# Short sorting networks drawn as two-dimensional passes, key segments stored side by side, and one subtraction left out, in a two-layer graph kernel

## The chip, the cores and the metric

The kernel runs on one core of a Trainium2 chip. The metric is device time in microseconds (us) of one execution, so lower is better. "VectorE" below is the engine that the profile calls DVE, "GpSimd" is POOL, "ScalarE" is ACT, "TensorE" is PE, and SyncE (SP) issues the plain transfers.

## The reference, cut to what matters

There are 16 graphs of 1024 nodes with 64 channels each, a weighted adjacency matrix per graph, and a node mask.

```python
# layer 0: mean over the neighbours, weighted by the adjacency
h = relu(layernorm(x));  x = x + (adj / clip(adj.sum(-1), 1)) @ h
# layer 1: a sum of quantiles over the neighbours that are left
h = relu(layernorm(x))
nb = (adj > 0) off the diagonal;  m = nb.sum(-1)
# a node with m > 10 drops every ceil(m/2)-th neighbour, and the drop goes both ways
sv = sort over the left neighbours and the node itself, per channel, of h
agg = 0.25*quantile(sv, .25) + 0.5*quantile(sv, .5) + 0.25*quantile(sv, .75)
x = x + mask * (relu((h + agg) @ W1 + b1) @ W2 + b2)
```

The number of neighbours is very uneven: the first nodes of a graph have the most, up to some 90, and most nodes have fewer than ten.

## The kernel before, in words

**Layer 0** goes batch by batch, 16 times. SyncE loads adjacency tiles of 128x1024 (`at`). ScalarE takes their signs (`sg`, with row sums), TensorE transposes them and multiplies them with the normalised rows. VectorE multiplies the signs by descending column numbers and takes the 8 largest out of each of 4 segments with MAX8 (`rec`), so each node gets a list of at most 32 neighbours. The stream `endings` then sorts the 1024 nodes of a batch by class of length. The class is a one-hot tile `hot`; two matmuls put into PSUM, for each of 184 columns (23 classes by 8 tiles), how many nodes stand earlier in the tile and how many the column has; a running sum over the columns (TENSOR_TENSOR_SCAN into `base`), a subtraction that makes it exclusive, an addition, a product with `hot` and a reduction give each node's position. GpSimd scatters the node's row to that position in DRAM (`srt<-row,to`).

**Layer 1** works on four groups of four batches. In a group the sorted positions are 32 tiles of 128 nodes; tile 0 holds the longest, and the others take the first `CAPS` neighbours: 15, 10, 8, 7, 7, 6, and so on down to 1. Tiles of one length form a job (`Job`): n = cap + 1 rows to sort (the node itself is row 0), T tiles. The jobs of a group have (n, T) = (16,1), (11,1), (9,1), (8,2), (7,1), (6,4), (5,4), (4,6), (3,6), (2,5). GpSimd gathers the n - 1 neighbour rows, one DMA_INDIRECT of 128 rows each (`places<-tab,idx`; in the last group `last_idx`). VectorE marks dropped neighbours and sorts each channel with a network of elementwise min and max over whole rows of 64 columns: the `passes`. Only the lower three quarters of the sorted rows are needed. Then `weigh` multiplies the rows by their weights into `prod`, TensorE sums them and runs the two small matrix products, and GpSimd scatters the result (`out_dram<-y`).

A network is not done in place. Every row has two copies: copy 0 in the gathered SBUF tile `places`, copy 1 in a PSUM tile `other` (row 0 starts in a third, `S`). For each comparator a digit of a hand-kept table `GOES[n]` says into which copies its minimum and its maximum go. `network` collects the comparators of a layer that have the same operation, the same source copies, the same distance and the same destination copy, and a cover function packs their rows into passes: `runs_of` into arithmetic runs (one stride), `grids_of` into grids of two strides with at most `MOST` = 8 rows. Grids are used in layers with a rule from `GOES_LONG`, which the long lists have and the short jobs do not. `spread` orders the passes so that one that needs a fresh result is put later. The tile framework adds a semaphore wait wherever an instruction conflicts with an earlier one on a tile. There is one buffer of `other`, so the passes of two short jobs never mix.

**Long lists.** The first positions of each group hold nodes with 88, 28, 21 and 18 kept neighbours. For each of these four lists `long_lists` gathers full adjacency rows (`gat_rows`), builds one f16 key per column (`lkey`, 128x1024), takes 16 or 24 keys out of each of 8 segments with MAX8 and MATCH_REPLACE8 (`lfound`), then the largest of those (`lkeys`). Segment s is every eighth column from s on, and the key tile is stored in column order, so a segment is read with a stride of 8 elements (16 bytes). Its rows then go through networks of n = 89, 29, 22 and 19 (`lplaces`, with `l0other` or `lother` as the second copy, both in SBUF).

**Order of the work.** Nearly everything is emitted at build time by a planner (`Plan`): streams offer their next instruction with a rank, the planner keeps a clock per engine with assumed costs, and the stream that can begin earliest on its engine goes next, ties by rank. The order on VectorE and GpSimd is the emitted one. A VectorE pass is assumed to take 0.07 us plus 1.04 ns per column; a wait between two passes is not in these costs. `progress["ahead"]` counts gathers that are planned and not yet emitted; while it is under 16, sorts are put ahead of layer 0's VectorE work so that gather buffers (four of `places`) come free. All these instructions carry line 240 in the profile, that of the helper that records them, so groups are told apart by tile.

Of the kernel before, what the change touches and what calls it, by code (L numbers as in the profile page):

```python
# [15 lines left out]
OP = mybir.AluOpType  # L16
# [28 lines left out]
LSEG = 8  # L45
# [80 lines left out]
def numbers(run):  # L126
# [7 lines left out]
    2: "2",  # L134
    3: "302",
    4: "03110",
    5: "130330222",
    6: "112302211333",
    7: "0331030103122000",
    8: "2112033030321122333",  # L140
    9: "211232203032203001023303333",
    11: "1212120202301300132300022233211111010",
    16: "12121212302030200303200130031332000333111131312202220111330033",
}


# [5 lines left out]
}  # L152


def network(n, width, block=None):

    count = -(-3 * (n - 1) // 4) + 1  # L160
    live = set(range(count))
    layers = []
    block = block or n
    for layer in reversed(SHORT.get(n) or batcher(n)):
        kept = [(i, j, i in live, j in live) for i, j in layer if i in live or j in live]
        live.update(x for pair in kept for x in pair[:2])
        layers.append(kept)
    goes = iter(GOES.get(n, ()))
    rules = iter(GOES_LONG.get(n, "").split())
    at = [2] + [0] * (n - 1)  # L170
    ops = []
    for layer in reversed(layers):
        kinds, after = {}, {}
        inside = all(i // block == j // block for i, j, _, _ in layer)
        rule = dict(zip(sorted({(at[i], at[j]) for i, j, _, _ in layer}), next(rules, "")))
        for i, j, lo, hi in layer:
            ai, aj = at[i], at[j]
            other = (0 if ai == 1 else 1) + (0 if aj == 1 else 2)
            to = int(rule.get((ai, aj)) or next(goes, other))
            results = [(OP.min, i, to & 1)] * lo + [(OP.max, j, to >> 1)] * hi  # L180

            results.sort(key=lambda r: r[2] == at[r[1]])
            after.update({i: 0, j: 0})
            for turn, (op, x, copy) in enumerate(results):
                part = i // block if inside else -(-n // block)
                kinds.setdefault((part, turn, op == OP.max, ai, aj, j - i, copy), []).append(i)
                after[x] = copy
        for x, copy in after.items():
            at[x] = copy
        for (part, _, is_max, *kind), left in sorted(kinds.items()):  # L190
            cover = grids_of if rule else runs_of
            ops.extend(
                (part, (OP.max if is_max else OP.min, *kind, run)) for run in cover(left)
            )
    parts = [
        spread([op for p, op in ops if p == part], width) for part in range(1 + -(-n // block))
    ]
    return parts, count, at
# [187 lines left out]
def list_path(ctx, tc, x, adj, nodemask, w1, b1, w2, b2, out, go):  # L386
    nc = tc.nc
    B, N, C = x.shape
# [47 lines left out]
    zeros = zero.to_broadcast([P, N])  # L436
# [75 lines left out]
    nc = plan.nc  # L512
# [238 lines left out]
    def endings(pool, now):  # L751

        first = lambda rank: rank - 3000
        for b, st in enumerate(batch):
            now[0] = b
            g = max(g for g in range(NG) if FIRST[g] <= b)
            size = GROUPS[g]
            yield "ACT", lambda: known(st, "rec", "row") if st["listed"] == NT else INF
            rec, total, row = st["rec"], st["total"], st["row"]

            for t in range(NT):
                nc.scalar.activation(
                    row[:, t, R0:R0 + 8 * NSEG], rec[:, t, :], AF.Relu, bias=before[:, t:t + 1]
                )


            yield "DVE", always
            found = new(pool, [P, NT, 8 * NSEG], BF, "found", 1)
            nc.vector.tensor_scalar(found, rec, 0.0, None, op0=OP.is_gt)
            d = new(tiny, [P, NT], F32, "d", 2)  # L770
            nc.vector.tensor_reduce(d, found, AX.X, OP.add)
            full = new(tiny, [P, NT], F32, "full", 2)
            nc.vector.tensor_reduce(
                full, found.rearrange("p t (s e) -> p t s e", e=8)[:, :, :, 7], AX.X, OP.max
            )
            nc.vector.scalar_tensor_tensor(d, full, float(STEPS[0]), d, op0=OP.mult, op1=OP.max)
            nc.vector.tensor_scalar(d, d, float(STEPS[0]), None, op0=OP.min)
            for s in STEPS[1:]:
                nc.vector.scalar_tensor_tensor(d, total, float(s), d, op0=OP.is_gt, op1=OP.add)
            free(rec)  # L780
            free(total)
            hot = new(tiny, [P, CLS, NT], BF, "hot", 2)
            nc.vector.tensor_tensor(
                hot, cls, d.unsqueeze(1).to_broadcast([P, CLS, NT]), OP.is_equal
            )
            yield "PE", lambda: max(at(hot), room("ps_small", 3))
            pc = new(ps_s, [P, HALF], F32, "ps_small", 3, users=1)
            K = CLS * NT
            flat = hot.rearrange("p c t -> p (c t)")
            nc.tensor.matmul(pc[:, :K], earlier, flat, start=True, stop=True)  # L790
            nc.tensor.matmul(pc[:, K:2 * K], ones, flat, start=True, stop=True)
            yield "DVE", lambda: at(pc) + SLACK
            base = new(tiny, [P, K], F32, "base", 2)
            nc.vector.tensor_tensor_scan(
                base, pc[:, K:2 * K], zeros[:, :K], 0.0, op0=OP.add, op1=OP.add
            )
            nc.vector.tensor_tensor(base, base, pc[:, K:2 * K], OP.subtract)
            nc.vector.tensor_tensor(base, base, pc[:, :K], OP.add)
            free(pc)
            nc.vector.tensor_tensor(base, base, flat, OP.mult)  # L800
            pos = new(tiny, [P, NT], F32, "pos", 2)
            nc.vector.tensor_reduce(pos, base.rearrange("p (c t) -> p t c", t=NT), AX.X, OP.add)
            low = new(tiny, [P, NT], I32, "low", 2)
            nc.vector.tensor_copy(low, pos)
            nc.vector.tensor_scalar(low, low, LSUB - 1, None, op0=OP.bitwise_and)
            if size == 2:
                aside = new(tiny, [P, 2, NT], F32, "aside", 2)
                for e, by in enumerate((-32.0, 64.0)):
                    nc.vector.tensor_scalar(
                        aside[:, e, :], pos, 64.0 / (e + 1), by, op0=OP.is_lt, op1=OP.mult  # L810
                    )
                for e in range(2):
                    nc.vector.tensor_tensor(pos, pos, aside[:, e, :], OP.add)
            nc.vector.tensor_scalar(
                pos, pos, float(size), float(LSUB * (b - FIRST[g])), op0=OP.mult, op1=OP.add
            )
            to = new(pool, [P, NT], I32, "to", 2)
            nc.vector.scalar_tensor_tensor(to, low, float(1 - size), pos, op0=OP.mult, op1=OP.add)
            for t in range(NT):
                yield "POOL", lambda: max(at(to), at(row)) + LOOSE if "normed" in st else INF, first  # L820
                scatter(srt[g], row[:, t, :], to[:, t:t + 1], sorts[g])
            free(row)
            progress["batches"] = b + 1
# [21 lines left out]
    class Job:  # L845
# [190 lines left out]
        def sort(self):  # L1036
            n, T, pool, short, A, S = self.n, self.T, self.pool, self.short, self.A, self.S
# [10 lines left out]
                ok, self.keys.rearrange("p t k -> p k t"), 0.0, gone, op0=OP.is_gt,  # L1048
                op1=OP.subtract,
            )  # L1050
            self.ops, self.count, self.copies = network(n, T * C)
            self.counts(ok)

            vals = A[:, 1:, :, :].rearrange("p k t w -> p (k t) w")[:, :, :C]
# [5 lines left out]
                HUGE, vals, op0=OP.mult, op1=OP.add,  # L1060
# [263 lines left out]
    def long_lists(pool):  # L1324

        yield "DVE", always
        rev = new(pool, [P, N], HF, "rev", 1)
# [13 lines left out]
        for l in LORDER:  # L1341
            K = LONG[l]
# [21 lines left out]
                full, col_f, node, full, op0=OP.not_equal, op1=OP.mult  # L1364
            )
            key = new(pool, [P, N], HF, "lkey", 1)
            nc.vector.scalar_tensor_tensor(key, full, 0.0, rev, op0=OP.is_gt, op1=OP.mult)

            found = new(pool, [P, LSEG, max(LCAPS)], HF, "lfound", 1)
            found = found[:, :, :LCAPS[l]]  # L1370
# [1 line left out]
            for r in range(LCAPS[l] // 8):  # L1372
                for s in range(LSEG):
                    if s % 4 == 0:
                        yield "DVE", always
                    top = found[:, s, 8 * r:8 * r + 8]
                    seg = key.rearrange("p (q s) -> p s q", s=LSEG)[:, s, :]
                    if r:
                        nc.vector.match_replace(
                            out=seg, in_to_replace=last[s], in_values=seg, imm_value=0.0  # L1380
                        )
                    nc.vector.max(out=top, in_=seg)
                    last[s] = top
# [89 lines left out]
    nc = tc.nc  # L1473
# [291 lines left out]
```

## Time and profile before

| | |
|---|---|
| Median of 3 runs | 1470.73 us (1468.12 to 1472.69) |
| The profiled execution's own time | 1469.38 us |
| Its span, first to last instruction | 1467.6 us |
| VectorE busy | 1267.8 us (86%), 4263 instructions |
| GpSimd busy | 939.3 us (64%), 1112 instructions |
| ScalarE, TensorE busy | 577.8 us, 738.8 us |
| Mean granted TensorE clock | 0.707 |

Busy time counts an instruction from its start to its end. Consecutive VectorE instructions can overlap, and the short idle time that a wait between two of them leaves is not in the busy share. On GpSimd the profile's busy time of a gather is about 1 us, and another 0.3 us between two gathers is shown as idle with releaser "issue".

### The profile page before, as it was taken

Reading aid. Unit: us, or ns where it says so; the run is one execution under the profiler, and the core shown is the slowest. Engines: PE = TensorE matmul, PEld = TensorE weight load, DVE = VectorE, ACT = ScalarE, POOL = GpSimd, SP = SyncE. Lnnn points to the kernel's source line nnn. Section 1 sums busy time; section 2 is a strip of 40 time slices with the busy share of each in tenths; the row PEclk is TensorE's granted clock in tenths of the full one; section 3 lists DMA queues with packets and bytes.
Section 4 is the critical chain, followed back from the end, with each engine's and each line's share of the span. In section 5 each row is a group of like instructions: output and inputs, shape, how many; then the busy total and the mean of one; then the engine's idle time right before and its main releaser. Section 6 shows DMA issues by size and latency. Waiting matters only on the chain.

```text
span 1467.6 us, 14957 instructions
## 1 busy us (share of the span) xinstructions
PE 738.8 (50%) x3186; PEld 460.6 (31%) x3186; DVE 1267.8 (86%) x4263; ACT 577.8 (39%) x1747; POOL 939.3 (64%) x1112
## 2 busy tenths in 40 slices
PE   4778777228778347683585663200510101224864
PEld 2444334214445224352353332100410001123753
DVE  6878799999999895899959967588999998999895
ACT  7989879245666324783454432000100000000110
POOL 0132227777767777577876777477777787778432
PEclk9889898559989558895598676555665555555876
DMA  5446667424464224465233232321211111221000
GB/s 175 150 145 185 163 192 196 119 67 112 135 164 141 66 51 112 129 194 136 69 93 96 82 71 48 63 68 41 43 39 24 25 30 31 44 46 24 16 11 11
DMA packets 134591, 132.22 MB, mean 90 GB/s; under 512 B 100196, under 2 KB 102884, under 8 KB 134372
## 3 DMA queue, kind: packets, MB, share of 16 engines
q1 hardware_dynamic: 102972, 91.00, 21.6%
q0 software_dynamic: 31520, 40.19, 12.6%
q14 instruction: 72, 0.59, 0.1%
q8 instruction: 27, 0.44, 0.1%
HBM read 111.62 MB, written 23.61 MB: 92 GB/s over the span
## 4 chain that ended last, share of the span: by engine, by line
DVE 44%; POOL 19%; issue 11%; ACT 10%; DMA 9%; PE 5%; SPq 1%; DVEq 0%; POOLq 0%; ACTq 0%
POOL places L240 11%; DVE places L240 7%; DVE other L240 6%; DVE lplaces L240 5%; DVE rec L240 5%; DMA at<-in_adj_dram 4%; DMA places<-tab,idx 4%; POOL lplaces L240 4%; ACT sg L240 3%; PE pt L240 3%; ACT ln_sq L240 2%; DVE l0other L240 2%; DVE sg L240 2%; POOL out_dram L240 2%; PE ps_small L240 2%
## 5 line engine op out<-in xcount | busy, mean ns | idle before, releaser
L240 POOL DMA_INDIRECT places<-tab,idx x372 | 371.6, 999 | 115.5 <-issue 105.7
L240 PE MATMUL pt<-ident,prod 128*128 128x128 f32 (+1 forms) x736 | 162.5, 384 | 396.4 <-DVE prod L240 320.3
L240 PEld LDWEIGHTS pt<-ident,prod 128*128 128x128 f32 (+1 forms) x736 | 132.9, 264 | 428.1 <-issue 255.7
L240 PE MATMUL ps_small<-att,h 128*65 128x512 f32 x512 | 255.0, 645 | 14.1 <-ACT att L240 6.7
L240 POOL DMA_INDIRECT srt<-row,to x128 | 128.1, 1001 | 178.5 <-ACT row L240 156.0
L240 PE MATMUL pt<-ident,at 128*128 128x128 f32 x1024 | 167.1, 308 | 93.9 <-ACT att L240 71.7
L240 DVE MAX8 rec<-sg 128x8 f16<-128x256 f16 x512 | 180.2, 414 | 4.4
L240 PEld LDWEIGHTS pt<-ident,at 128*128 128x128 f32 x1024 | 128.0, 156 | 139.0 <-ACT att L240 95.3
L240 ACT ACTIVATE sg<-at 128x1024 f16<-128x1024 f32 x128 | 135.0, 1055 | 89.9 <-DMA at<-in_adj_dram 69.6
L240 POOL DMA_INDIRECT lplaces<-whole,lidx x125 | 132.1, 1057 | 38.3 <-issue 37.4
L240 POOL DMA_INDIRECT places<-tab,last_idx x124 | 126.2, 1018 | 37.8 <-issue 36.3
L240 ACT COPY att<-pt 128x512 f32<-128x512 f32 x256 | 141.4, 583 | 19.0 <-PE pt L240 17.6
L240 PEld LDWEIGHTS ps_small<-att,h 128*65 128x65 f32 x512 | 74.0, 151 | 148.2 <-issue 119.7
L240 ACT COPY ot<-pt 128x128 f32<-128x128 f32 (+3 forms) x56 | 22.4, 399 | 230.2 <-PE pt L240 228.1
L240 DVE TENSOR_TENSOR sg<-sg,keyed 128x1024 f16<-128x1024 f16 x128 | 87.3, 682 | 29.4 <-ACT sg L240 29.3
L240 POOL DMA_INDIRECT out_dram<-y,nodes_i x93 | 97.0, 1043 | 21.0 <-issue 13.9
L240 ACT ACTIVATE wu<-wu 128x39 f32<-128x39 f32 (+9 forms) x40 | 9.5, 237 | 255.2 <-DVE wu L240 255.2
L240 PE MATMUL ps_small<-ot,w_sb 128*128 128x128 f32 (+3 forms) x112 | 49.4, 531 | 100.4 <-DVE y L240 84.1
L240 ACT ACTIVATE hid<-ps_small,b_sb 128x128 f32<-128x128 f32 (+2 forms) x56 | 28.1, 504 | 126.3 <-PE ps_small L240 126.0
L240 DVE TENSOR_TENSOR other<-places,other 128x64 f32<-128x64 f32 (+6 forms) x204 | 69.4, 340 | 5.4
L240 DVE TENSOR_TENSOR places<-places,other 128x64 f32<-128x64 f32 (+2 forms) x208 | 62.3, 309 | 4.8
L240 DVE TENSOR_TENSOR places<-other,places 128x128 f32<-128x128 f32 (+5 forms) x160 | 54.9, 343 | 3.4
(269 smaller groups left out, 1651.3 us busy)
## 6 DMA issues: line engine op xcount, KB each, us to landing
at<-in_adj_dram SPq DMA_DIRECT2D x128, 512.0 KB
places<-tab,idx POOLq DMA_INDIRECT x372
whole<-tab SPq DMA_DIRECT2D x4, 1057.0 KB
tab<-row SPq DMA_DIRECT2D x16, 264.0 KB
xt<-in_x_dram SPq DMA_DIRECT2D x16, 256.0 KB
srt<-row,to POOLq DMA_INDIRECT x128
lplaces<-whole,lidx POOLq DMA_INDIRECT x125
places<-tab,last_idx POOLq DMA_INDIRECT x124
```

The lines of the kernel that those rows point to most:

```text
L240: ins = getattr(self._engine, op)(*args, **kwargs)
```

## The change

1. Five tables of `GOES` are new (n = 5, 7, 9, 11, 16): the min and max results of the comparators go to other copies than before.
2. For jobs of one tile (T = 1: n = 16, 11, 9, 7) `network` covers with `grids_of` in place of `runs_of`. The networks themselves, their comparators and the rows that they compare are the same. The lists of n = 29, 22, 19 go through the same call with `one` true; their passes stay as they are.
3. The long lists' key tile is written segment by segment, so that a segment's 128 keys are contiguous; the one instruction that writes the keys of a list now writes with a stride of 128 elements (256 bytes) from one key to the next.
4. In `endings` the scan starts one column later, behind a MEMSET of the first column, which makes the sum exclusive without the subtraction.

```diff
-    5: "130330222",
+    5: "110013113",
-    7: "0331030103122000",
+    7: "2110003230211333",
-    9: "211232203032203001023303333",
-    11: "1212120202301300132300022233211111010",
-    16: "12121212302030200303200130031332000333111131312202220111330033",
+    9: "121220200011112221230000333",
+    11: "1212101010001222211000022211100003333",
+    16: "12121212010301030000222022201111000000222222220000111111000000",
...
-def network(n, width, block=None):
+def network(n, width, block=None, one=False):
...
-            cover = grids_of if rule else runs_of
+            cover = grids_of if rule or one else runs_of
...
             base = new(tiny, [P, K], F32, "base", 2)
+            nc.vector.memset(base[:, :1], 0.0)
             nc.vector.tensor_tensor_scan(
-                base, pc[:, K:2 * K], zeros[:, :K], 0.0, op0=OP.add, op1=OP.add
-            )
-            nc.vector.tensor_tensor(base, base, pc[:, K:2 * K], OP.subtract)
+                base[:, 1:], pc[:, K:2 * K - 1], zeros[:, :K - 1], 0.0, op0=OP.add, op1=OP.add
+            )
             nc.vector.tensor_tensor(base, base, pc[:, :K], OP.add)
...
-            self.ops, self.count, self.copies = network(n, T * C)
+            self.ops, self.count, self.copies = network(n, T * C, one=T == 1)
...
             key = new(pool, [P, N], HF, "lkey", 1)
-            nc.vector.scalar_tensor_tensor(key, full, 0.0, rev, op0=OP.is_gt, op1=OP.mult)
+            segs = key.rearrange("p (s q) -> p s q", s=LSEG)
+            nc.vector.scalar_tensor_tensor(
+                segs.rearrange("p s q -> p q s"), full.rearrange("p (q s) -> p q s", s=LSEG), 0.0,
+                rev.rearrange("p (q s) -> p q s", s=LSEG), op0=OP.is_gt, op1=OP.mult,
+            )
...
-                    seg = key.rearrange("p (q s) -> p s q", s=LSEG)[:, s, :]
+                    seg = segs[:, s, :]
```

## The prediction

> **What bounds the kernel now.** I read the page's first two parts, then busy time by stage, then the vector engine's timeline inside one short job, then the rows of single tiles.
>
> ```profile
> PE 738.8 (50%) x3186; PEld 460.6 (31%) x3186; DVE 1267.8 (86%) x4263; ACT 577.8 (39%) x1747; POOL 939.3 (64%) x1112
> ...
> DVE  6878799999999895899959967588999998999895
> ACT  7989879245666324783454432000100000000110
> POOL 0132227777767777577876777477777787778432
> ...
> DVE 44%; POOL 19%; issue 11%; ACT 10%; DMA 9%; PE 5%; SPq 1%; DVEq 0%; POOLq 0%; ACTq 0%
> ```
>
> VectorE is busy nearly everywhere and carries 44% of the chain that ended last. GpSimd's 7s are not slack: between two gathers lie 0.3 us with the releaser "issue", so a gather costs 1.25 to 1.3 us and at most 39 fit into 50 us. Three stages by window:
>
> ```profile
> 200.00:915.00 715.00, 433.53 (x1848) 262.13 (x1847) 623.73 (x2102) 363.81 (x1105) 529.13 (x639) 0.76 0.42 112
> 915.00:1380.00 465.00, 107.63 (x499) 81.90 (x498) 416.93 (x1330) 26.70 (x70) 347.75 (x359) 0.56 0.19 39
> 1380.00:1467.60 87.60, 50.02 (x257) 39.96 (x256) 70.66 (x254) 9.83 (x26) 24.53 (x41) 0.71 0.03 10
> ```
>
> The waits of GpSimd have this row:
>
> ```profile
> POOL out_dram L240 <- DVE lrem L240: 22.9, 1, 22.9
> ```
>
> In the windows the columns are PE, PEld, DVE, ACT, POOL. In 200 to 915 (layer 0 with groups 0 to 2) VectorE is 87% busy; with its short waits between dependent instructions only some 50 us of the 715 are real idle. In 915 to 1380 (long lists, group 3) it is 34 of 465. GpSimd is full too: leaving out gaps under 0.4 us, it idles 58 us in all from 250 to 1375. But its last gather is issued at 1378, and then VectorE still has 71 us of sorting; the wait shows GpSimd standing 22.9 us for it. So the end is VectorE's backlog, with GpSimd close behind.
>
> **Where a short sort spends its time.** The timeline of VectorE in group 2's n = 16 job (start, us, instruction; "x2" are two merged):
>
> ```profile
> 768.79 0.30 DVE L240 TENSOR_TENSOR other<-places 128x128 f32<-128x128 f32 x1
> 769.13 0.22 DVE L240 TENSOR_TENSOR places<-other,places 128x64 f32<-128x64 f32 x1
> 769.27 0.47 DVE L240 TENSOR_TENSOR places<-places,other 128x128 f32<-128x128 f32 x2
> 769.78 0.23 DVE L240 TENSOR_TENSOR other<-other,places 128x64 f32<-128x64 f32 x1
> 770.04 0.29 DVE L240 TENSOR_TENSOR places<-places,other 128x128 f32<-128x128 f32 x1
> ```
>
> From 769.13 to 769.27 a 64-column pass takes 0.14 us, from 769.78 to 770.04 it takes 0.26. A free pass costs 0.07 us plus 0.067 per row of 64; one that waits for its predecessor starts 34 ns after that one's end and costs 0.12 more. I marked every pair of neighbouring passes in the 40 short jobs. A pass waits when it reads or writes `other` and the pass before it wrote `other`, or writes it and that one read it, **whatever the rows** (the PSUM tile is tracked as a whole); in `places` only when the rows themselves conflict. Of 605 pairs marked as conflicting 578 wait, of 195 marked free none does.
>
> [...]
>
> **Part 1, networks.** I worked the old and new tables through `network` and `spread`, counted passes, and waits by the rule above. Rows moved are unchanged (17, 31, 52, 72, 121 rows times T). Time is 0.07 x passes + 0.067 x rows x T + 0.12 x waits.
>
> | n (T) | passes | waits | us by rule | saved |
> |---|---|---|---|---|
> | 5 (4) | 16 to 14 | 13 to 9 | 7.2 to 6.6 | 0.6 |
> | 7 (1) | 22 to 20 | 16 to 12 | 5.5 to 4.9 | 0.6 |
> | 9 (1) | 38 to 29 | 28 to 20 | 9.5 to 7.9 | 1.6 |
> | 11 (1) | 43 to 32 | 30 to 19 | 11.4 to 9.3 | 2.1 |
> | 16 (1) | 63 to 36 | 51 to 21 | 18.6 to 13.1 | 5.5 |
>
> The trace has 18.9, 10.4 to 10.9, and 9.0 to 9.4 us for n = 16, 11, 9 before, so the rule is sound; where another job's instruction falls between two passes it hides a wait, and I take 40 us for four groups in place of 41.6. The rows' final copies also need fewer `prod` products: one less for n = 5, 9, 11, two for n = 16, at 0.07 us, 1.4 us in all. That a two-stride pass costs no more per row is read from the long lists, where such passes of 512 columns take 685 ns, as one-stride ones do; none touches PSUM yet. There are 24 two-stride passes a group. Below, they cost nothing more (each row is still 64 contiguous columns), or gain; above, take the 13 ns by which 64-column passes on `other` alone last longer than on `places` first (232 against 219), 96 times: 1.2 us. I take nothing.
>
> **Part 2, keys.** The rows of the tile (min/median/max ns):
>
> ```profile
> L240 DVE MAX8 lfound<-lkey x72: 364/384/395, 958.7 to 1082.1; 128x8 f16<-128x128 f16 x72
> L240 DVE MATCH_REPLACE8 lkey<-lfound,lkey x40: 706/709/726, 961.0 to 1081.4; 128x128 f16<-128x128 f16 x40
> L240 DVE MAX8 lkeys<-lfound x25: 284/296/361, 978.9 to 1084.8; 128x8 f32<-128x128 f16 x13, 128x8 f32<-128x192 f16 x12
> L240 DVE MATCH_REPLACE8 lfound<-lkeys,lfound x21: 274/341/343, 979.4 to 1084.5; 128x192 f16<-128x192 f16 x11, 128x128 f16<-128x128 f16 x10
> L240 DVE SCALAR_TENSOR_TENSOR lkey<-gat_rows,rev x4: 1224/1224/1225, 957.4 to 1070.1; 128x1024 f16<-128x1024 f32 x4
> ```
>
> The same two instructions stand in the trace on contiguous f16 of the same width: MATCH_REPLACE8 276 ns against 710, MAX8 294 against 384. (The list's MAX8 at an 8-byte stride, 409 ns for 256 columns, pays nothing[...].) Saved: 40 x 0.434 + 72 x 0.090 = 23.8 us; all of it is serial, since each waits for the one before.
>
> The price is the key write, now 256 bytes from element to element. No row shows such a write. Below: nothing. Above: put the whole surplus of MATCH_REPLACE8, 434 ns / 128 = 3.4 ns per element, on its write: 1024 x 3.4 = 3.5 us, four times, 13.9. MAX8's surplus, 0.7 ns per element, is reading alone; the rest, 2.7, is the write if the two add up, and part of it overlaps with the 1.04 that the element costs anyway. I take 2.25 us each, 9 in all. Net 15.
>
> **Part 3, subtraction.** `base<-base,ps_small` lasts 345 ns and with its wait 380. One of two goes, 16 times: 6.1 us. The MEMSET's nearest row (`idle`, 59 ns) starts 25 ns after its predecessor and doesn't delay the next; at worst 16 x 0.06 = 1 us. I take 5.5.
>
> **The sum and the path.** 40 + 1.4 + 15 + 5.5 = 62 us less VectorE time (54 to 73 with the bounds). From 915 on lie the keys (15) and group 3 (10.3): 25 us, all on the backlog. Before 915 lie three groups (31) and the subtraction (5.5). There VectorE bounds too, but it then meets layer 0's other waits sooner (29.3 us for `sg`, 21.0 for `deg` over the span), and GpSimd's pace of 190 indirect transfers a group, 243 us, which group 1 already follows group 0 by (239). I let three quarters through: 28 us. Sum 53. The profiled execution is 1469.4, 1.35 below the median: 1469.4 - 53 = 1416, median **1418**.
>
> No transfer, gather or matmul is added or removed. VectorE now waits next for gathers: GpSimd finishes at 1378 less what it idles, so about 1350, plus 20 us for the last job's sort, products and scatters. The end cannot fall far under 1390.
>
> **Rivals.** (a) GpSimd sets the pace before 915: its slices are full there, and only part 2 and group 3 count: 25 to 30 us, 1441 to 1446. Against it stand its 36 us of idle before 900, nearly all in front of `srt`, `gat_rows` and `tab`, which wait for layer 0 and the group's lists. (b) The waits stay, because two-stride passes on PSUM are tracked worse: 48 more waits a group, 23 us back, 39 left, 33 on the path: 1438. (c) **Slower**: the emitted order turns. Shorter passes move the planner's clocks; if at 953 to 1211 it puts group 3's 124 gathers ahead of the long lists' 125, VectorE loses the 57 us of long-list passes that fill 1211 to 1380 now, and they follow at the end: 1418 + 57 = 1475, slower once more than 53 us of filler is lost. Against it: long lists have the better rank (-600 to 300), and their keys come sooner. (d) The key write costs all of its bound and more: still faster, about 1423.
>
> **Numbers.** The forecast 72%, (a) with (b) 20%, (c) 5%, in between and without measurable effect 3%. About 0.3% (4.4 us) is what a measurement can tell from no change. Range 1394, with every part at its best bound and all of it on the path (1398) less one measurement's width, to 1448, which takes in (a) and (b).
>
> **What would show it.** Passes of n = 16 from 18.9 to about 13 us; MATCH_REPLACE8 on `lkey` near 276 ns, MAX8 near 294; the key write between 1.2 and 4.7 us; VectorE busy near 1220; its work after the last gather down from 71 to under 45 us. Wrong: waits at every pass of the new jobs, or GpSimd without idle from 250 to the end.

## The result: 12 us in place of 53

The changed kernel takes 1457.25 us (median, 1455.76 to 1457.91), the kernel before in the same comparison 1469.42: ratio 0.9919 with a 95% interval of 0.9896 to 0.9942. The profiled execution has a span of 1456.0 us, 11.6 less than before. The forecast was 1418. On some chips every kernel, before too, took 20 to 30% longer; times from there stand apart.

The page of the changed kernel, busy times, the slices of three engines, and the shares of the chain that ended last:

```profile
PE 745.0 (51%) x3186; PEld 463.6 (32%) x3186; DVE 1214.5 (83%) x4039; ACT 579.9 (40%) x1747; POOL 960.6 (66%) x1120
...
DVE  6868798997989968899766874868999979999885
ACT  7989978444656527672353830000000010001110
POOL 0132227777767887677778576577777877777754
...
DVE 36%; POOL 22%; issue 11%; PE 10%; DMA 10%; ACT 9%; SPq 0%; DVEq 0%; POOLq 0%; ACTq 0%
```

VectorE is busy 53.3 us less than before (1267.8). Its gaps of up to 60 ns between instructions, where the short waits are, fell from 62.4 to 53.7 us. Together that is 62 us less, as the sum of the prediction had it. But its idle stretches of over 60 ns grew from 129.7 to 180.1 us: of the 62 us, 50 turned into waiting and 12 shortened the kernel. The POOL row is as full as before, and POOL's share of the chain went from 19 to 22%. The three stages (us, PE, PEld, DVE, ACT, POOL, then clock, DMA share and GB/s):

```profile
200.00:915.00 715.00, 432.12 (x1813) 258.33 (x1811) 589.47 (x1970) 364.94 (x1103) 524.67 (x637) 0.75 0.43 114
915.00:1380.00 465.00, 121.18 (x538) 93.08 (x538) 414.02 (x1286) 28.10 (x77) 361.19 (x351) 0.56 0.18 35
1380.00:1456.10 76.10, 45.79 (x253) 35.98 (x252) 55.60 (x201) 9.29 (x23) 36.77 (x59) 0.72 0.05 16
```

Before 915 VectorE works 34 us less (623.7 before), and in this stretch that is waiting. Its longest waits now (total, times, longest):

```profile
DVE sg L240 <- ACT sg L240: 48.3, 16, 12.7
DVE rem L240 <- DMA places<-tab,idx: 23.6, 6, 9.5
DVE gat_rows L240 <- DMA gat_rows<-in_adj_dram,lnodes_i: 20.0, 3, 12.9
...
DVE rev L240 <- DMA srt<-row,to: 17.6, 1, 17.6
```

The same four before:

```profile
DVE sg L240 <- ACT sg L240: 29.3, 12, 8.7
...
DVE rem L240 <- DMA places<-tab,idx: 11.4, 5, 3.6
DVE gat_rows L240 <- DMA gat_rows<-in_adj_dram,lnodes_i: 10.9, 3, 5.6
...
DVE rev L240 <- DMA srt<-row,to: 8.3, 1, 8.3
```

They grew by 50 us in all. The second, third and fourth are waits for GpSimd's transfers.

Taken from the list of GpSimd's instructions in both traces, from the first gather to the last (a pause over 0.4 us counts as idle):

| us | before | after |
|---|---|---|
| first gather starts | 213.9 | 213.3 |
| indirect transfers in between, duration | 856.5 (837) | 868.3 (829) |
| pauses up to 0.4 us between instructions | 233.1 | 231.9 |
| idle | 57.8 | 51.5 |
| other small instructions | 18.2 | 18.2 |
| last gather ends | 1379.5 | 1383.2 |
| from there to the end of the span | 88.1 | 72.8 |
| VectorE busy in that tail | 71.2 | 52.6 |

This table is the result. The last gather did not move forward; only the tail behind it is 15 us shorter. Layer 0 did end 35 us sooner (last `srt` scatter at 886.6, before at 921.2), but at 887 us both kernels have the same 370 indirect transfers left, 349 of them up to the last gather before and 341 now. From 887 on to the end of the last gather the kernel before needs 492 us, of which GpSimd idles 22; the changed one 496 with 19. Its two longest pauses around the turn to the last group (total, times, longest; 640 to 1060 us) did not shrink:

```profile
POOL gat_rows L240 <- DVE gfound L240: 16.1, 1, 16.1
...
POOL srt L240 <- ACT row L240: 13.5, 5, 12.7
```

Before, in the same window:

```profile
POOL gat_rows L240 <- DVE gfound L240: 14.8, 1, 14.8
...
POOL srt L240 <- ACT row L240: 10.4, 2, 10.2
```

With layer 0's earlier end the first of them only moved forward, its end from 951 to 920 us; the second ends at 816, before at 813.

**Inside a short job** the change does what was forecast. VectorE in group 2's n = 16 job, where two-stride passes now carry four rows and more:

```profile
755.14 0.69 DVE L240 TENSOR_TENSOR places<-places 128x256 f32<-128x256 f32 x2
755.75 0.22 DVE L240 TENSOR_TENSOR places<-S,places 128x64 f32<-128x64 f32 x1
755.89 0.41 DVE L240 TENSOR_TENSOR places<-other,places 128x256 f32<-128x256 f32 x1
756.34 0.43 DVE L240 TENSOR_TENSOR other<-places,other 128x256 f32<-128x256 f32 x1
```

From 755.75 to 755.89 a pass without a wait, from 755.89 to 756.34 one with it (34 ns lie open after it). The keys (min/median/max ns):

```profile
L240 DVE MAX8 lfound<-lkey x72: 274/294/296, 930.4 to 1046.9; 128x8 f16<-128x128 f16 x72
...
L240 DVE MATCH_REPLACE8 lkey<-lfound,lkey x40: 273/276/281, 932.1 to 1046.6; 128x128 f16<-128x128 f16 x40
L240 DVE SCALAR_TENSOR_TENSOR lkey<-gat_rows,rev x4: 4699/4703/4715, 925.7 to 1036.1; 128x1024 f16<-128x1024 f32 x4
```

The cheap readers came as read from the other rows; the key write costs the whole upper bound, 3.48 us more each. And it does something that was in no step. GpSimd in the changed kernel around the first key write:

```profile
923.43 0.94 POOL L240 DMA_INDIRECT places<-tab,idx  x1 [0.30 <-issue]
924.68 1.80 POOL L240 DMA_INDIRECT places<-tab,idx  x1 [0.30 <-issue]
926.79 3.94 POOL L240 DMA_INDIRECT places<-tab,idx  x1 [0.30 <-issue]
931.03 0.95 POOL L240 DMA_INDIRECT places<-tab,idx  x1 [0.31 <-issue]
```

VectorE in the same stretch:

```profile
924.38 1.28 DVE L240 SCALAR_TENSOR_TENSOR gat_rows<-col_f,lS,gat_rows 128x1024 f32<-128x1024 f32 x1 [4.97 <-DMA gat_rows<-in_adj_dram,lnodes_i]
925.70 4.70 DVE L240 SCALAR_TENSOR_TENSOR lkey<-gat_rows,rev 128x1024 f16<-128x1024 f32 x1
```

A gather that starts during either instruction lasts until after that instruction's end. All four key writes have such a gather (3.94, 3.94, 3.95, 3.88 us in place of 0.945): 3.0 us each, 12 in all. The table's second row is 11.8 us longer with 8 transfers fewer, so a transfer takes 1.047 us on average in place of 1.023, which is 20 us over 829 transfers; 12 of these are the key writes.

### The profile page after: what moved, and what is told of

The parts are those of the page before. It is cut to its first block, busy times and chain, and to the rows that moved or that the text cites. A ratio compares the mean times of both kernels' runs of the same rounds, so it can differ in the third digit from the quotient of the medians.

```text
span 1456.0 us, 14752 instructions
## 1 busy us (share of the span) xinstructions
PE 745.0 (51%) x3186; PEld 463.6 (32%) x3186; DVE 1214.5 (83%) x4039; ACT 579.9 (40%) x1747; POOL 960.6 (66%) x1120
## 3 DMA queue, kind: packets, MB, share of 16 engines
q0 software_dynamic: 31520, 40.19, 12.8%
## 4 chain that ended last, share of the span: by engine, by line
DVE 36%; POOL 22%; issue 11%; PE 10%; DMA 10%; ACT 9%; SPq 0%; DVEq 0%; POOLq 0%; ACTq 0%
POOL places L240 14%; DVE places L240 6%; PE ps_small L240 5%; PE pt L240 5%; DMA at<-in_adj_dram 5%; DVE lplaces L240 4%; DVE other L240 4%; DVE rec L240 4%; DMA places<-tab,idx 3%; POOL out_dram L240 3%; ACT sg L240 3%; DVE l0other L240 3%; POOL lplaces L240 2%; ACT ln_sq L240 2%; DVE sg L240 2%
## 5 line engine op out<-in xcount | busy, mean ns | idle before, releaser
L240 POOL DMA_INDIRECT places<-tab,idx x372 | 375.5, 1009 | 114.5 <-issue 106.7
L240 DVE MAX8 rec<-sg 128x8 f16<-128x256 f16 x512 | 180.1, 414 | 4.4
L240 POOL DMA_INDIRECT lplaces<-whole,lidx x125 | 145.4, 1164 | 38.1 <-issue 36.9
L240 POOL DMA_INDIRECT places<-tab,last_idx x124 | 133.5, 1077 | 37.8 <-issue 35.7
L240 ACT COPY att<-pt 128x512 f32<-128x512 f32 x256 | 142.0, 583 | 18.9 <-PE pt L240 16.9
L240 POOL DMA_INDIRECT out_dram<-y,nodes_i x93 | 94.0, 1010 | 22.3 <-issue 13.3
L240 DVE TENSOR_TENSOR places<-places,other 128x128 f32<-128x128 f32 (+6 forms) x160 | 56.3, 354 | 3.3
L240 PE MATMUL ps_small<-w_sb,hid 128*128 128x64 f32 x256 | 51.8, 343 | 7.1 <-ACT hid L240 6.8
L240 DVE TENSOR_TENSOR places<-other,places 128x128 f32<-128x128 f32 (+5 forms) x136 | 48.7, 365 | 1.7
```

What stands on the lines that cost most here:

```text
L240: ins = getattr(self._engine, op)(*args, **kwargs)
```

## The theories

**P**: GpSimd's stream of gathers sets the end. VectorE's savings count only in the tail, and in so far as they let GpSimd idle less; what lengthens gathers costs in full (**K**: the key write does). **V**: VectorE's time counts as forecast, and something else ate the gain. **O**: the planner reorders with the new passes (an own price and fewer of them), and the 12 us are the order's luck.

In what follows "before" is the kernel before on the same chip in the same comparison.

## Experiments: one part at a time

**Keys alone.** The kernel before with part 3 of the change only; the planner's prices see no difference, so the order is that of before.

```diff
-            nc.vector.scalar_tensor_tensor(key, full, 0.0, rev, op0=OP.is_gt, op1=OP.mult)
+            segs = key.rearrange("p (s q) -> p s q", s=LSEG)
+            nc.vector.scalar_tensor_tensor(
+                segs.rearrange("p s q -> p q s"), ...
```

> The kernel before with the key segments side by side alone. Theory P (GpSimd's stream of gathers sets the pace; a gather that meets a VectorE instruction with two SBUF inputs is held until that one ends, and four key writes of 4.7 us hold four gathers by 3 us each): VectorE does 9 us less, GpSimd 12 us more, so no gain, 1468 to 1480. Theory V (VectorE's time counts as the prediction had it, only smaller): 9 us faster, about 1460.

Measured: 1477.5 us against 1469.7, ratio 1.0045 (1.0024 to 1.0066). VectorE is busy 9.0 us less (1258.8), the gathers last 14.2 us more (870.7), the kernel is 7 to 8 us **slower**. V falls here: saved VectorE time did not pay, lost GpSimd time did.

**Networks alone**, parts 1 and 2 of the change on the kernel before:

> The kernel before with the new tables and grids alone. VectorE does about 46 us less in either theory. P: the last gather is issued at about 1365 to 1380 as before, VectorE's idle time takes most of the 46 us, and only the part after the last gather shrinks: 1448 to 1460. V: 40 us faster, 1430.

Measured: 1466.6, ratio 0.9975 (0.9963 to 0.9987), a smaller gain than either theory said. The planner made another order here, with the last gather at 1401.7 and 81 us of GpSimd idle.

**All but the keys** (the changed kernel with the old key write and the old reads; the emitted order is the changed kernel's):

> The changed kernel with the old key layout (networks and subtraction stay). VectorE does 9 us more than in the changed kernel. P: no gather is held for 3.9 us any more, GpSimd does 10 us less, so it is faster than the changed kernel although VectorE has more to do: 1443 to 1452. V: 7 to 9 us slower than the changed kernel, 1465.

Measured: 1453.7, ratio 0.9887 (0.9862 to 0.9912), 1.7 us above P's forecast and some 5 us faster than the changed kernel (0.9919 above, 0.9928 in its second comparison below), though VectorE is busy 11 us more (1225.8). This kernel and the one before it differ by a subtraction of 0.35 us, 16 times, and by the order; they stand 13 us apart. So an order can be worth up to some 13 us, and theory O needed a test that keeps it.

**Keys read apart, written together.** The changed kernel, with the stride of 8 elements on the f32 input in place of the 256 bytes on the f16 output; `rev` is stored in segment order. The emitted order is the changed kernel's.

```diff
             nc.vector.scalar_tensor_tensor(
-                segs.rearrange("p s q -> p q s"), full.rearrange("p (q s) -> p q s", s=LSEG), 0.0,
-                rev.rearrange("p (q s) -> p q s", s=LSEG), op0=OP.is_gt, op1=OP.mult,
+                segs, full.rearrange("p (q s) -> p s q", s=LSEG), 0.0,
+                rev.rearrange("p (s q) -> p s q", s=LSEG), op0=OP.is_gt, op1=OP.mult,
```

> The changed kernel, but the key tile is written contiguously in segment order and the stride of 8 elements is on the reads (the descending column numbers are stored in segment order once). The key write should last 1.9 us (1.2 plus 0.7 ns per element of one strided read) in place of 4.7. P: 11 us less on VectorE and 11 us less on GpSimd's gathers, 1443 to 1449. V: 2 to 4 us faster only, about 1454, since 11 us of VectorE time would be worth what 62 us were (one fifth).

Measured: 1450.6, ratio 0.9873 (0.9848 to 0.9898). The write lasts 1.99 us (1.22 before, 4.70 in the changed kernel), the gathers at it 1.67 to 1.69. That is 1.6 us above P's forecast, 3.4 under V's, and faster than both kernels.

## Experiments: the same order, and fewer gathers

To keep the order, the planner is told of the old instructions and the new ones are emitted in their places. GpSimd's whole sequence is then that of before, and on VectorE only the changed instructions differ; ScalarE's, TensorE's and SyncE's, which the framework orders, differ among neighbours (108 places of 1747 on ScalarE, 83 of 3186 on TensorE).

```diff
-            for op, ai, aj, dist, copy, run in self.ops[part]:
+            for turn, (op, ai, aj, dist, copy, run) in enumerate(planned, 1):
...
-                nc.vector.tensor_tensor(dst, a, c, op)
+                plan.note("DVE", "tensor_tensor", (dst, a, c, op), {})
+                while (sent + 1) * len(planned) <= turn * len(real):
+                    ...
+                    raw.vector.tensor_tensor(...)
+                    sent += 1
```

The second edit takes every fourth gather of a job off GpSimd, 103 of them (54 of 372, 18 of 124, 31 of 125), with the order kept:

```diff
+                    if k % 4 == 3:
+                        plan.note("POOL", "indirect_dma_start", ...)
+                        raw.sync.dma_start(A[:, k + 1, t, :], self.table[:P, :])
+                    else:
                         gather(A[:, k + 1, t, :], self.table, self.idx[:, t, k:k + 1])
```

New instructions in the old order:

> The changed kernel's instructions in the order of the kernel before: the planner is charged the old passes, products and subtraction, so GpSimd's whole sequence is that of before, and on VectorE only the changed instructions differ. Theory P (GpSimd's stream of gathers sets the end, the key writes hold it up, VectorE's savings count only behind the last gather): the tail of 88 us shrinks by some 18, the four held gathers give 0 to 12 back, so 1452 to 1462 us. Theory O (what the changed kernel gained, it gained by its new emitted order): 1467 to 1472, no gain. Theory V (VectorE's time counts): about 1410.

Old instructions in the new order:

> The instructions of the kernel before (old passes, products, keys in column order, subtraction) in the order of the changed kernel. Theory P: the tail is back, the held gathers are gone: 1463 to 1475 us. Theory O: the gain of the changed kernel stays, 1455 to 1459. Theory V: about 1520.

The lightened kernel before, and the lightened kernel with the new instructions in the old order:

> The kernel before in its own order, but every fourth gather of a job (k = 3, 7, 11 and so on) is a plain transfer of the first 128 rows of the table by SyncE, so its output is not the reference's; about a hundred gathers, some 130 us, are off GpSimd. Theory P: VectorE becomes the bound; its busy time and waits are 1330 us and it can't start at once or sort what has not landed, so 1390 to 1430 us. Theory V: VectorE was the bound already, so it stays within 20 us of 1469. Theory O has no number of its own here, since the order is kept.

> The changed kernel's instructions in the order of the kernel before, with every fourth gather of a job a plain transfer as in the lightened kernel before; output not the reference's. Theory P: with GpSimd no longer the pace, VectorE's 62 us less come through nearly whole: 45 to 62 us under the lightened kernel before, 1335 to 1380 us. If the savings are worth little for another reason (in-order waits, the emitted order), the gap stays at 5 to 20 us as with all gathers.

These four met a chip on which before took 1910 us. They gave 1824.5, 1860.3, 1780.0 and 1683.9 us. In those profiles GpSimd stands 396 to 500 us between its gathers and VectorE 413 to 539, at a mean granted TensorE clock of 0.66 to 0.67 in place of 0.70; TensorE shows pauses that belong to nothing in the profile (`PE pt L254 <- issue` in the kernel with the old instructions in the new order: 126.6 us, 39 times, the longest 12.0). Neither engine bounds there, and even the old instructions in the new order gained 50 us, so the runs don't speak on the question as it stands where before takes 1470; why that chip was slower stays open. Three were repeated:

> Once more the changed kernel's instructions in the order of the kernel before, since in the first such runs every kernel, before too, took 30% longer and GpSimd stood 400 us. Where before takes about 1470 us: theory P (GpSimd's gathers set the end) 1452 to 1462 us, theory O (the gain is the new emitted order's) 1467 to 1472, theory V (VectorE's time counts) about 1410.

> Once more the kernel before with every fourth gather of a job a plain transfer of the first 128 rows of the table by SyncE (output not the reference's), 103 gathers less on GpSimd. Where before takes about 1470 us: theory P 1390 to 1430 us, VectorE being the bound then; theory V, in which it was the bound already, 1450 to 1469.

> Once more the changed kernel's instructions in the order of the kernel before, with every fourth gather of a job a plain transfer (output not the reference's). Theory P: with GpSimd off the path, VectorE's 62 us less come through nearly whole, 45 to 62 us under the lightened kernel before. If savings on VectorE are worth little for another reason, the gap is 5 to 20 us.

with before at 1471.7 us:

| | all gathers | 103 gathers fewer |
|---|---|---|
| old instructions | 1471.7 | 1449.7 (0.9854, 0.9830 to 0.9878) |
| new instructions, same order | 1463.8 (0.9953, 0.9929 to 0.9976) | 1402.8 (0.9540, 0.9519 to 0.9562) |

This shows the cause. In the old order the new instructions save VectorE 54 us with all gathers and 56 with fewer (busy time and gaps of up to 60 ns; 62 in the changed kernel, whose order hides more of the waits). **Nearly the same saving brings 8 us with all gathers and 47 with fewer.** With all gathers VectorE's idle stretches of over 60 ns grow by 48 us (129.7 to 177.8), with fewer by 9 (109.8 to 118.7). When the plain transfers land is not shown; both kernels of the right column have them in common. Equally, 103 gathers fewer bring 22 us alone and 61 with the new instructions. Together they bring 69 where the two alone add up to 30: each engine was full behind the other. Not all of P's numbers came: the new instructions with all gathers stand 1.8 us above its 1452 to 1462 and under O's range, and the lightened kernel before missed its 1390 to 1430 and stands at the lower edge of V's 1450 to 1469, since VectorE was nearly as full as GpSimd. P by itself says too little: both engines were full. The lightened kernel's page:

```profile
PE 747.4 (52%) x3186; PEld 464.1 (32%) x3186; DVE 1267.1 (88%) x4263; ACT 580.3 (40%) x1747; POOL 836.5 (58%) x1010
...
DVE  6878799999999996889969967598999999999895
...
POOL 0132218747667757566876677476577773567332
```

With the new instructions as well:

```profile
PE 738.8 (53%) x3186; PEld 459.1 (33%) x3186; DVE 1218.7 (87%) x4039; ACT 580.2 (41%) x1747; POOL 851.2 (61%) x1010
...
DVE  6878789999999996899969966696999999999995
...
POOL 0022317767667777576876687477677775667333
```

Between its first and last gather GpSimd idles 58 us in the kernel before, 172 in the lightened one, 110 with the new instructions as well. So in the lightened kernel GpSimd waits more, and the savings on VectorE cut these waits by 62 us.

**The order by itself.** The changed kernel once more, and the old instructions in its order, with before at 1469.8:

> The changed kernel itself, on the same chip as the next three: 1455 to 1460 us, as before, if before takes about 1470.

> Once more the instructions of the kernel before in the order of the changed kernel. Where before takes about 1470 us: if the order gave the changed kernel's gain, 1455 to 1460; if the instructions gave it (theory P: a shorter tail behind the last gather), 1463 to 1475.

Measured: 1459.6 (0.9928, 0.9912 to 0.9943) and 1477.2 (1.0053, 1.0038 to 1.0068). The second is 2 us above P's forecast and far from O's. Theory O falls as the main cause: with the old instructions the new order is 7 us worse than the old, not better. The new instructions bring 18 us in the new order and 8 in the old. With the new instructions the new order is 4 us better than the old (0.9928 against 0.9953, the intervals overlap), so up to a third of the 12 us may belong to the order and the instructions together.

## Experiments: what the key write costs

To part the write's own time from the held gathers, the key was made in two instructions in the changed kernel's order: a comparison with the 256-byte stride and one SBUF input, then a contiguous f16 product.

```diff
+            raw.vector.tensor_scalar(
+                segs.rearrange("p s q -> p q s"), full.rearrange("p (q s) -> p q s", s=LSEG),
+                0.0, None, op0=OP.is_gt,
+            )
+            raw.vector.tensor_tensor(key, key, rev, OP.mult)
```

> The changed kernel with its key in two instructions: a comparison with the 256-byte stride (one SBUF input) and a contiguous f16 product in place, in the same emitted order. VectorE has 2 to 3 us more to do. If the dear write costs because a VectorE instruction with two SBUF inputs holds GpSimd's gathers: no gather over 2 us at the comparison, 5 to 12 us under the changed kernel, 1445 to 1452. If it costs by its own 3.5 us on VectorE: the same or up to 3 us over the changed kernel.

Measured: 1453.2, ratio 0.9898 (0.9878 to 0.9918): faster than the changed kernel, but not for the reason given. VectorE of this kernel:

```profile
1001.21 2.45 DVE L1373 TENSOR_SCALAR lkey<-gat_rows 128x1024 f16<-128x1024 f32 x1
1003.69 0.69 DVE L1377 TENSOR_TENSOR lkey<-lkey,rev 128x1024 f16<-128x1024 f16 x1
```

and its GpSimd:

```profile
1001.15 2.63 POOL L240 DMA_INDIRECT lplaces<-whole,lidx  x1 [0.30 <-issue]
1004.08 1.12 POOL L240 DMA_INDIRECT lplaces<-whole,lidx  x1 [0.30 <-issue]
```

The comparison ran in half of 4.70 us, and the gather was held by it all the same, to 0.12 us after its end; so it is at all four comparisons, with gathers of 2.63 to 3.60 us. "One input" was the wrong mark. In the changed kernel a TENSOR_SCALAR over 1024 columns (`gfound<-gat_rows`) takes 0.69 us; with `skip` as second input and its sum written out as well it takes 1.27 to 1.28, and the six gathers that run beside such instructions take 0.94 to 0.95 us each. That the halved time and the held gathers go together was the author's estimate from these. So the comparison was given such a sum (`op1=OP.add, accum_out=some`):

> As key_one, but the comparison with the 256-byte stride also writes out its sum over the columns (accum_out), the form that elsewhere in this kernel left its gathers at 943 ns. Expected of the comparison: about 4.7 us, with gathers of 945 ns under it; VectorE then has some 3 us more to do than in the changed kernel (1459 us). If the held gathers are the cost of the dear write: 1447 to 1454 us. If its own time on VectorE is: 1459 to 1463.

> Once more the comparison with the 256-byte stride that also writes out its sum, 4.70 us with gathers of 944 ns under it, and the contiguous product of 0.69 us after it; some 4 us more VectorE work than in the changed kernel. Where before takes about 1470 us and the changed kernel 1459: if the held gathers are the cost of the dear write, 1447 to 1454; if its own time on VectorE is, 1459 to 1463.

> The same kernel a last time, for its time where the kernel before takes about 1470 us and the changed kernel 1459: if the held gathers are the cost of the dear key write, 1447 to 1454; if its own time on VectorE is, 1459 to 1463.

The first two met chips on which before took 1910 and 1877 us (ratios 0.9596 and 0.9777); the last gave 1451.4, ratio 0.9885 (0.9863 to 0.9908). Its VectorE and its GpSimd:

```profile
928.20 4.69 DVE L1374 TENSOR_SCALAR_CACHE_REDUCE lkey<-gat_rows 128x1024 f16<-128x1024 f32 x1
932.52 0.37 DVE L1374 DVE_READ_ACCUMULATOR lkey<-gat_rows 128x1 f32 x1
932.93 0.69 DVE L1378 TENSOR_TENSOR lkey<-lkey,rev 128x1024 f16<-128x1024 f16 x1
```

```profile
927.24 1.74 POOL L240 DMA_INDIRECT places<-tab,idx  x1 [0.30 <-issue]
929.28 0.94 POOL L240 DMA_INDIRECT places<-tab,idx  x1 [0.31 <-issue]
930.53 0.94 POOL L240 DMA_INDIRECT places<-tab,idx  x1 [0.30 <-issue]
931.78 0.94 POOL L240 DMA_INDIRECT places<-tab,idx  x1 [0.30 <-issue]
```

The same stride and the same 4.7 us, and three gathers pass under it unhindered (the first one shown is still held by the instruction ahead of it). VectorE is busy 2.3 us more than in the changed kernel (1218.1 against 1215.8), the gathers last 12.4 us less (855.2 against 867.6), and the kernel is 6 to 8 us faster: 1451.4 against 1459.6 and 1457.25 in the changed kernel's two comparisons on other chips (ratio 0.9885 against 0.9928, intervals apart, and 0.9919, intervals overlapping by 0.0012). With the run of all but the keys this shows K: the dear write costs by holding GpSimd.

**A planner that knows the waits**, with the key of the run with keys read apart:

```diff
+                    if self.short and waits:
+                        plan.clock["DVE"] += 0.12
```

(`waits` stands for the rule of the prediction: a conflict with the pass before on rows of `places`, or on `other` as a whole.)

> The changed kernel with the key written contiguously (as in the run with keys read apart, 1451 us) and a planner that is charged 0.12 us for each pass that must wait for its predecessor; only the emitted order differs from that run. A better order by true costs: 1435 to 1447. If the order is as good as chance: 1440 to 1465.

Measured: 1454.0, ratio 0.9904 (0.9882 to 0.9926): no better order than the changed kernel's own with the same key (0.9873), as "good as chance" had it. Of the kernels that make all gathers, the keys read apart have the lowest time (1450.6); the comparison with the sum (1451.4) is within the noise of it.

## Why the prediction was wrong

- **The rule of waits and the table: right.** Where nothing falls between the passes, in two n = 16 jobs of the new instructions in the old order, a job takes 13.2 and 13.3 us with 21 waits: the forecast was 13.1 and 21, and before it took 18.9. There the passes of n = 11 take 8.8 to 9.3 us where the job isn't held up (forecast 9.3), n = 9 7.5 to 8.0 (7.9), n = 5 6.3 to 6.8 (6.6). In the changed kernel 19 to 33 instructions of other work stand between the passes of an n = 16 job; 14 to 17 waits are left, and its own passes take 11.8 to 12.8 us.
- **The keys: readers right, the write mis-sized.** It was taken at 2.25 us more each, within 0 to 3.48; it measured 3.48. VectorE's own net was then 9 to 11 us in place of 15.
- **The sum: 62 us came, in part by luck.** In the old order the new instructions save 54 to 56 us, since the keys bring less than forecast; that the new order hides more of the waits, some 7 us, was not forecast.
- **The step that failed is the path**: "25 us on the backlog" after 915 and "three quarters" of 37 before it, 53 in all, where 12 came and 50 us turned into VectorE's waiting. It took the 71 us that VectorE still had to do after the last gather as proof that VectorE bounded the end, and GpSimd as "close behind". The four kernels of the same order, with all gathers and with fewer, show two full engines. VectorE keeps the emitted order and can't do early what has not been gathered, so the time saved before a gather turns into a wait for it (48 of 54 us in the same order with all gathers), and the backlog shrinks only by what is saved behind the last one (71.2 to 52.6 us).
- **"GpSimd finishes at about 1350 plus 20 us"** rested on half of its idle going away. It lost 6 of 58 us, since its longest pauses wait for a chain of short steps (the last group's lists, the rows that ScalarE completes) and not for the mass of VectorE's work (this is read from the timelines; no run tests it). The 12 us of held gathers, which were in no step, came on top.
- **The rivals.** (a) had the right engine and the wrong place: GpSimd's pace was given to the stretch before 915 alone, hence 1441 to 1446. After 915, where the windows showed VectorE at 90% (417 of 465), GpSimd had no more to give: 22 us of idle from 887 to its last gather. (b) falls with the waits. (c) falls: the order did turn, but the other way, with the long lists' gathers from 974 to 1172 us and group 3's all behind them, and it cost the old instructions 7 us. (d) came true on VectorE up to its bound; the held gathers were in no rival.
- **What was to show it**: the passes, MATCH_REPLACE8, MAX8 and VectorE's busy time came as listed; its work after the last gather, forecast under 45, is 52.6, and that one line told of the path. Neither of the two signs of being wrong came: the new jobs don't wait at every pass, and GpSimd still idles 51 us. It set the pace all the same: VectorE's savings took out only 6 of its 58 us.

## What to carry to other kernels

When two engines that keep the emitted order are both nearly full, price a saving on the first by the idle that it can take out of the second, stage by stage, and by its own work behind the second's last instruction: here at most 22 us after layer 0, of which 3 came, and some 18, whatever VectorE saved. And weigh a long VectorE instruction also by what it keeps from others: under the key write with two SBUF inputs GpSimd's gathers took 3.88 to 3.95 us in place of 0.945, under the comparison 2.63 to 3.60, and under the comparison that also writes out its sum 0.94.

## What was not expected of the hardware

- In the changed kernel 40 indirect transfers start under a VectorE instruction of over 1 us with two SBUF inputs, 0.2 us or more before its end. Four of them, at the strided key writes, end 0.32 to 0.33 us after that instruction's end, the other 36 0.75 to 0.87 us after it, whatever their own 0.945 us: one takes 4.96 us at the product `lplaces<-lplaces,l0w` of 4.55 us. In the kernel before, three that start within 0.07 us after the start of such an instruction take 0.94 to 0.98 us. Of the gathers that start under a product of over 1 us in the changed kernel, the eight under `prod<-other,w`, where one input is in PSUM, that start 0.2 us or more before its end take 0.95 us, and the four under `prod<-places,w`, with both in SBUF, that start 0.7 us or more before its end 1.52 to 1.95; two that start in its last 0.23 us take 0.96 and 1.05. Which part of a transfer is held, no run shows.
- f16 written 256 bytes apart costs 4.70 us for 1024 elements, contiguous 1.22; f32 read 32 bytes apart and f16 written contiguously 1.99. A TENSOR_SCALAR with the same 256-byte write takes 2.45 us, and 4.69 once it also writes out its sum.
